# Row scores of a graph-attention layer: from transposes on TensorE to block turns on VectorE and a spread through memory, with new orders of the steps

## The chip, the core and the metric

The kernel runs on one core of a Trainium2 chip. The metric is the device time of one execution in microseconds, the median of five runs. Matrix products run on TensorE (PE; its weight loads are PEld), elementwise work on VectorE (DVE), ScalarE (ACT) and GpSimd (POOL); SyncE (SP) issues nearly all DMAs, in the order of its program. Every engine works through its own instructions in order and waits where an operand or a buffer isn't ready.

## What is computed

The input is x, 128 graphs of 128 nodes with 512 features, and a weighted adjacency adj per graph. Two layers follow each other, each with a residual. Cut to what matters:

```
h = relu(layernorm(x))                                # layer 0: attention over the graph
q, k, v = h Wq^T + bq, h Wk^T + bk, h Wv^T + bv       # 8 heads of 64
attn = softmax(q k^T / 8 * (adj + adj))               # per head, over keys
x = x + (attn v) Wo^T + bo
h = relu(layernorm(x))                                # layer 1: graph attention
Wh = h W
e = leaky_relu(Wh a[:512] + (Wh a[512:])^T, 0.2)      # a row score plus a column score
att = softmax(where(adj > 0.5, e, -9e15), axis=1)     # over the first index
x = x + elu(att Wh)
```

All is float32.

## The kernel before

Graphs go through in 64 pairs. For layer 0 two pairs make a group of four graphs; the projections q, k and v of a group are done with seven products instead of eight (a 2x2 block scheme: sums of token blocks and of weight blocks, `PRODUCTS`), called v0 to v6, q0 to q6, k0 to k6 and spread as "units" U1 to U11 over the two pairs before. A unit is four 128x128 by 256 matmuls (L249). Their results are moved out of PSUM by F (ACT, copy or bias) and A (DVE, add). Then, for each graph of a pair (suffix a and b): sc, the scores (L311); at, the weighting with adj (L318); mx, ex, rc, nm, the softmax; fl, bl, pl, which turn the shares in 32x32 blocks on DVE (L346), write them to memory and fetch them back in turned places (SP, L350 and L356); pc, the context (L375). o0 to o6 are the seven products of the output projection (L290), od their adds to x (L389).

Layer 1 of a pair: st (statistics, L159), pw (EPS and the power -0.5 on POOL, L163 and L164), nm and h2 (normalised h, L405), then four dot products per pair (L412): d00 and d10 give the row score of each node of the two graphs, d01 and d11 the column score, each against a vector of 512 (`us_sb`, `ut_sb`) that is W times one half of a, worked out once. The mask step needs, on every partition, the row scores of all 128 nodes along the free dimension. So pb (L421) turns the score column, broadcast to 128 columns, against the identity on TensorE, one transpose per graph, and wm (L427) reads pb in PSUM beside adjT. pr (leaky), m1, e1, sw finish the softmax; g0, g1 gather (L453), w0 to w6 are the products with W (L290), zc and wd collect them; ez, fa, fb (L476, L479, L482) make the elu and the residual over both graphs of the pair at once, so (L485) stores 512 KB.

Once, at the start: five weights of 1 MB each are loaded by one DMA each (Lv, Lq, Lk, Lo, Lw, L622), their block sums are made on DVE (W..0 to W..3, L134 to L140); bo and the two halves of a are loaded as rows broadcast to all partitions (Lc, Lu0, Lu1). ccp (L494) multiplies Wo with bv, broadcast to 128 columns, ccd adds bo: a constant row c that sh adds to x (L225). The first four pairs get their h by normalising rows (hn) and turning them on TensorE (tp, L188; ev, ACT). The biases bq, bk, bv come as columns on ACT's DMA queue.

No planner runs at build time. The order in which all engines' instructions are issued is written out in three lists: HEAD (first pairs, every step with its pair), ORDER (one period of the pairs 3 to 59; "pb:2" is the step pb of the pair two before the current one) and TAIL (last pairs, counted from the end). Each engine gets its instructions in the order of these lists, and SP its DMAs: a DMA that waits holds back all that stand behind it.

Of the kernel before, what the change touches and what calls it, by code (L numbers as in the profile page):

```python
# [13 lines left out]
P = 128  # L14
# [5 lines left out]
Q = 32  # L20
# [4 lines left out]
def kernel(  # L25
# [86 lines left out]
    bv_sb = column(bv, "bv")  # L112

# [3 lines left out]
    c_sb, us_sb, ut_sb = (const.tile([P, E], F32, name=name) for name in ("c", "u_src", "u_dst"))  # L117

    def load_row(dst, src, offset=0):
        nc.sync.dma_start(dst, bass.AP(tensor=src.tensor, offset=src.offset + offset, ap=[[0, P], [1, E]]))  # L120
# [32 lines left out]
    def row_stats(src, name):  # L153

        mv = small.tile([P, 2, 2], F32, name=name)

        def stats(i):
            st = small.tile([P, nc.vector.BN_STATS_DIM], F32, name="st")
            nc.vector.bn_stats(st, src[:, i, :])  # L159
            nc.vector.bn_aggr(mv[:, i, :], st)  # L160

        def power():
            nc.gpsimd.tensor_scalar_add(mv[:, :, 1], mv[:, :, 1], EPS)  # L163
            nc.gpsimd.tensor_tensor(mv[:, :, 1], mv[:, :, 1], mhalf.to_broadcast([P, 2]), OP.pow)  # L164

        return mv, stats, power
# [4 lines left out]
    def stats0(p, i):  # L171
        if p not in st0:
            st0[p] = row_stats(xs[p] if p < 3 else x0s[p], "mv0")
        st0[p][1](i)
# [185 lines left out]

    cxT = const.tile([P, 7, 2, S], F32, name="cxT")
# [34 lines left out]
    def centre1(p):  # L396
        mv = l1s[p][0]
        nmr = small.tile([P, 2], F32, name="nmr")
        nc.vector.scalar_tensor_tensor(nmr, mv[:, :, 0], -1.0, mv[:, :, 1], op0=OP.mult, op1=OP.mult)
        l1s[p] = mv, nmr  # L400
        h1s[p] = work.tile([P, 2, E], F32, name="h2"), small.tile([P, 2, 2], F32, name="ws")
# [7 lines left out]
    def dot1(p, i, k):  # L409
# [3 lines left out]
            junk, h2[:, i, :], 1.0, (us_sb, ut_sb)[k], op0=OP.mult, op1=OP.mult, accum_out=ws[:, i, k : k + 1]  # L413
        )

    def scores1(p):
        ws = h1s[p][1]

        pb = ps1.tile([P, 2, S], F32, name="pb", tag="ps1")
        for i in range(2):  # L420
            nc.tensor.transpose(pb[:, i, :], ws[:, i, 0:1].to_broadcast([P, P]), ident)  # L421
        pbs[p] = pb

    def mask1(p):

        wts[p] = work.tile([P, 2, S], F32, name="w", bufs=2)
# [7 lines left out]
    def maxima1(p):  # L434
        l1s[p] = small.tile([P, 2], F32, name="nmx1"), small.tile([P, 2], F32, name="sums1")
# [7 lines left out]
    def normalise1(p):  # L443
        w, (_, sums) = wts[p], l1s.pop(p)
        rs = small.tile([P, 2], F32, name="rs1")
# [27 lines left out]
    def elu(p):  # L473

        ezs[p] = work.tile([P, 2, E], F32, name="ez")
        nc.scalar.activation(ezs[p], zs[p], AF.Exp)  # L476

    def finish_a(p):
        nc.vector.scalar_tensor_tensor(xs[p], zs[p], 0.0, xs[p], op0=OP.max, op1=OP.add)  # L479

    def finish_b(p):
        nc.vector.scalar_tensor_tensor(xs[p], ezs.pop(p), 1.0, xs[p], op0=OP.min, op1=OP.add)  # L482
# [4 lines left out]
    ucol = const.tile([P, 2, C], F32, name="ucol")  # L487


    def product_c():  # L490
        onces["c"] = pm = ps1.tile([P, 2, E // 2], F32, name="pm", tag="ps1")
        for f in range(2):
            for c in range(C):
                nc.tensor.matmul(  # L494
                    pm[:, f, :], bv_sb[:, c : c + 1].to_broadcast([P, P]), wo_sb[:, 2 * (c // 2) + f, c % 2, :],
# [3 lines left out]
    def sum_c():  # L499
        pm = onces["c"].rearrange("p f k -> p (f k)")  # L500
        nc.vector.scalar_tensor_tensor(c_sb, pm, -1.0, c_sb, op0=OP.add, op1=OP.add)


    def dots_u(i, half):
        junk = work.tile([P, E], F32, name="junk")
        for c in (2 * half, 2 * half + 1):
            nc.vector.scalar_tensor_tensor(
                junk.rearrange("p (f k) -> p f k", f=2), w1_sb[:, 2 * half : 2 * half + 2, c % 2, :], 1.0,
                (us_sb, ut_sb)[i].rearrange("p (f k) -> p f k", f=2), op0=OP.mult, op1=OP.mult,
                accum_out=ucol[:, i, c : c + 1],  # L510
            )

    def turn_u(i):
        onces["u", i] = pu = ps1.tile([P, C, P], F32, name="pu", tag="ps1")
        for c in range(C):
            nc.tensor.transpose(pu[:, c, :], ucol[:, i, c : c + 1].to_broadcast([P, P]), ident)

    def keep_u(i):
        pu = onces["u", i].rearrange("p c k -> p (c k)")
        nc.scalar.activation((us_sb, ut_sb)[i], pu, AF.Copy, scale=1.0 if i else 1.0 / MASK)  # L520
# [11 lines left out]
    def listed(text, mark):  # L532
# [3 lines left out]
        lx@0 Lq@0 t0@-5 lx@1 Lo@0 Lk@0 Wq0@0 t1@-5 pp@0 t1@-4 lx@2 Lc@0 t0@-4 hn0@0 pp@1 Lv@0 hn1@0 tp0@0 Lw@0 tp1@0  # L536
        Lu0@0 ev0@0 hn1@1 ev1@0 hn0@1 tp1@1 Wq1@0 U6@-2 Wq2@0 tp0@1 ccp@0 ev0@1 t0@-3 F6@-2 t1@-3 ev1@1 Wk0@0 pp@2 l0@-2
        Wk2@0 la@-1 lt@0 Wk1@0 U5@-1 Lu1@0 hs2@-3 Wv0@0 hn0@2 U8@-2 ccd@0 hs0@-3 sh@0 U3@-1 t1@-2 tp0@2 F3@-1 la@0 U1@-1
        t0@-2 hs1@-3 pp@3 hn1@2 U7@-1 hs3@-3 hn0@3 hn1@3 U10@-2 cu01@0 F7@-1 l0@-1 ev0@2 Ww0@0 tp1@2 Wo0@0 U9@-1 ev1@2
        A8@-2 F10@-2 cu11@0 U1@-2 F9@-1 A5@-1 sh@1 tp0@3 U2@-1 tp1@3 F2@-1 U10@-1 ev0@3 A2@-1 ev1@3 hs0@-1 U4@-1 F10@-1  # L540
        Wv1@0 Wq3@0 t0@-1 U3@1 F4@-1 Ww1@0 hs1@-1 sca@0 t1@-1 scb@0 ata0@0 l0@0 s0@-1 ata1@0 U6@-1 mxa@0 Ww3@0 exa0@0
        U2@-2 Wv2@0 exa2@0 exa3@0 U8@-1 F1@-2 rca1@0 Wo2@0 nma2@0 exa1@0 U1@0 A9@-1 Wk3@0 rca0@0 t0@0 nma1@0 U3@-2
        nma3@0 A2@-2 nma0@0 t1@0 U4@-2 F3@-2 fla@0 l0@1 s0@0 f0@0 atb0@0 bla@0 U5@-2 atb1@0 Wv3@0 mxb@0 U11@-1 F5@-2
        exb3@0 U7@-2 A11@-1 exb1@0 A5@-2 exb0@0 cu00@0 U6@0 f0@1 pla@0 hs2@-1 Wo1@0 U2@0 F6@0 rcb0@0 A6@-1 F7@-2 exb2@0
        U9@-2 F1@0 rcb1@0 nmb3@0 F3@1 U10@0 A9@-2 lT@1 nmb2@0 cu10@0 nmb1@0 lT@0 sup0@0 scb@1 sua0@0 nmb0@0 sca@1 F10@0
        flb@0 U7@1 ata0@1 blb@0 ata1@1 A2@0 U5@1 F7@1 mxa@1 U9@1 Wo3@0 exa0@1 hd0@0 plb@0 exa2@1 exa1@1 pca@0 hs3@-1
        t0@1 U3@0 pea@0 rca0@1 hd1@0 nma1@1 exa3@1 U1@1 F3@0 rca1@1 t1@1 nma0@1 nma2@1 l0@2 s0@1 U2@1 nma3@1 la@1 fla@1
        U5@0 F2@1 atb0@1 bla@1 F9@1 hd0@1 o0@0 atb1@1 o1@0 mxb@1 pcb@0 pla@1 U4@1 peb@0 exb3@1 cs0@0 od0@0 exb1@1 cs1@0
        U8@0 A2@1 exb2@1 A5@1 exb0@1 cs2@0 U6@2 F5@0 A8@0 t0@2 t1@2 U4@0 od1@0 rcb1@1 rcb0@1 Ww2@0 nmb2@1 U8@1 nmb0@1
        nmb3@1 nmb1@1 U6@1 F4@1 flb@1 F6@2 hd1@1 U10@1 blb@1 hs0@1 cs3@0 o2@0 F10@1 A6@1 pca@1 od2@0 hs1@1 plb@1 sca@2  # L550
        pea@1 o4@0 ata0@2 ata1@2 o3@0 f0@2 od4@0 l0@3 mxa@2 U7@0 lt@1 od4c@0 A9@1 sup1@0 o5@0 sua1@0 exa1@2 o0@1 od5@0
        exa2@2 o1@1 exa0@2 o6@0 od0@1 st0@0 pcb@1 od6@0 st1@0 peb@1 scb@2 exa3@2 od1@1 pw@0 U11@1 cs0@1 rca1@2 rca0@2
        hs2@1 nma0@2 cs1@1 nma1@2 A5@0 s0@2 o2@1 nma2@2 nm@0 nma3@2 U1@2 F7@0 fla@2 h20@0 U9@0 atb0@2 F1@2 bla@2 h21@0
        atb1@2 mxb@2 U3@2 lT@2 A9@0 exb3@2 d00@0 exb2@2 U10@2 d01@0 pla@2 F3@2 od2@1 exb0@2 cs2@1 U5@2 hs3@1 A11@1 la@2
        d11@0 U4@2 F5@2 hd0@2 exb1@2 rcb1@2 rcb0@2 d10@0 o4@1 nmb3@2 nmb1@2 U8@2 od4@1 nmb2@2 A5@2 nmb0@2 flb@2 o3@1
        pb@0 U2@2 cs3@1 blb@2 od4c@1 wm@0 pr@0 U7@2 m1@0 o6@1 F7@2 plb@2 e1@0 o5@1 sw@0 U9@2 od6@1 hd1@2 g0@0 od5@1
        st0@1 g1@0 ge0@0 st1@1 A2@2
    """
    ORDER = """
        U1:0 A9:1 F10:1 pw:2 so:4 hs2:1 A1:8 ge1:3 F8:-4 gs0:3 w0:3 nm:2 w1:3 zc0:3 sca:0 F11:1 h20:2 wd1:3 gs2:3 scb:0  # L560
        h21:2 A4:8 ata0:0 ata1:0 pca:1 lx:1 hs1:1 pcb:1 mxa:0 pea:1 F1:0 U11:1 gs1:3 lT:0 exa1:0 A6:1 d00:2 U2:0 exa3:0
        d10:2 exa0:0 A8:1 d01:2 exa2:0 U3:0 rca0:0 d11:2 peb:1 nma0:0 A11:1 w2:3 rca1:0 F2:0 cs0:1 cs1:1 nma1:0 w3:3
        zc2:3 pb:2 nma2:0 U4:0 wm:2 nma3:0 cs2:1 A2:0 pr:2 gs3:3 F3:0 o0:1 fla:0 o1:1 atb0:0 bla:0 w4:3 A7:-9 A3:-1 m1:2
        f0:0 atb1:0 lt:1 U5:0 zc4:3 mxb:0 la:0 e1:2 sh:1 o3:1 wd4c:3 pla:0 w5:3 od0:1 od1:1 U6:0 zc5:3 F5:0 A10:7 A5:0
        exb2:0 sw:2 exb3:0 w6:3 exb0:0 rcb1:0 o2:1 wd6:3 exb1:0 cs3:1 g0:2 od2:1 nmb2:0 hs3:1 rcb0:0 nmb3:0 o4:1 fa:3
        nmb1:0 U7:0 nmb0:0 t1:0 ge0:2 od4:1 od4c:1 g1:2 F7:0 flb:0 ez:3 o5:1 blb:0 F6:0 o6:1 od5:1 F4:0 st0:1 U9:0 t0:0
        F9:0 od6:1 s0:0 U8:0 hd0:0 plb:0 hd1:0 U10:0 hs0:0 fb:3 st1:1 l0:-1
    """
    TAIL = """
        so@-8 w0@-7 F10@-5 A9@-5 pw@-6 w1@-7 hs1@-5 sca@-4 zc0@-7 ge1@-7 scb@-4 ata0@-4 lx@-5 nm@-6 pca@-5 ata1@-4  # L570
        h21@-6 gs0@-7 mxa@-4 pcb@-5 pea@-5 U6@-4 peb@-5 A6@-5 exa1@-4 gs1@-7 gs2@-7 exa3@-4 cs0@-5 hs2@-5 o0@-5 h20@-6
        o1@-5 exa0@-4 d01@-6 U3@-3 exa2@-4 wd1@-7 cs2@-5 rca1@-4 d10@-6 nma3@-4 w2@-7 d00@-6 F6@-4 rca0@-4 U8@-4 sh@-5
# [194 lines left out]
```

## Time and profile before

| what | us |
| --- | --- |
| median of five runs | 2367.5 (2366.54 to 2368.3) |
| the profiled execution | 2367.5 |
| its span, first to last instruction | 2365.7 |
| TensorE busy | 2339.8 |
| VectorE busy | 2005.5 |
| ScalarE busy | 1436.8 |
| row-score transposes pb, 128 of them, busy | 24.5 |
| share of the chain that ended last, on TensorE | 97% |

The page names a group of instructions by its line in the kernel, its engine, what it writes and what it reads. The busy time of matmuls contains their drain, which overlaps the next matmul, so a matmul's "mean ns" is longer than the time that it takes in a stream. The chain that ended last is followed back from the last instruction to whatever released each step; its durations are the times between steps.

### The profile page before, as it was taken

To read this page: it belongs to the slowest core of one execution; us is meant where nothing else is said; L and a number is where in the kernel's file an instruction comes from. 1 tells how busy PE (TensorE), PEld (TensorE's weight loads), DVE (VectorE), ACT (ScalarE), POOL (GpSimd) and SP (SyncE) were. 2 spreads that over 40 slices of the span, in tenths; PEclk is the share of its full clock that TensorE was granted. 3 is DMA by queue.
4 is the path that set the end of the run, shared out by engine and by line. 5 is a ranking of instruction groups with operands and counts; after the bars stand their busy time and mean duration, and the time that the engine had idled before them with its cause. 6 is when DMAs were issued, how large, how long until landed. Compare 5 with 4: busy or idle time off the path is not lost.

```text
span 2365.7 us, 40912 instructions
## 1 busy us (share of the span) xinstructions
PE 2339.8 (99%) x14264; PEld 2060.3 (87%) x14264; DVE 2005.5 (85%) x4037; ACT 1436.8 (61%) x4811; POOL 221.3 (9%) x323
## 2 busy tenths in 40 slices
PE   7999999999999999999999999999999999999997
PEld 6888888888888888888888888888888888888886
DVE  7788888888888888888888888888888888888887
ACT  3656566665566665655665666556656566665674
POOL 1000110101101101011011010010110100101000
PEclk9999999999999999999999999999999999999999
DMA  5445445444544454455454554544554545544432
GB/s 178 122 114 126 134 123 138 133 125 133 134 126 134 134 133 122 130 133 135 125 134 133 135 128 123 140 128 125 134 141 127 131 120 140 132 128 119 123 113 86
DMA packets 255277, 306.11 MB, mean 129 GB/s; under 512 B 21856, under 2 KB 181600, under 8 KB 254432
## 3 DMA queue, kind: packets, MB, share of 16 engines
q1 hardware_dynamic: 251568, 303.37, 46.7%
q8 instruction: 113, 1.85, 0.3%
q14 instruction: 92, 0.75, 0.1%
q0 software_dynamic: 1920, 0.13, 0.1%
q10 hardware_dynamic: 1584, 0.01, 0.0%
HBM read 202.64 MB, written 100.79 MB: 128 GB/s over the span
## 4 chain that ended last, share of the span: by engine, by line
PE 97%; DVE 2%; DMA 1%; issue 0%; ACT 0%; POOL 0%; SPq 0%; DVEq 0%; ACTq 0%; POOLq 0%
PE acc_a L249 28%; PE row_a L290 23%; PE acc_c L249 14%; PE row_c L290 9%; PE acc_b L249 7%; PE sc L311 5%; PE pc L375 5%; PE pg L453 5%; PE pb L421 1%; DMA wq<-in_wqT 0%; DVE junk L412 0%; PE pt L188 0%; DVE st L159 0%; DMA x<-in_x 0%; DVE x L482 0%
## 5 line engine op out<-in xcount | busy, mean ns | idle before, releaser
L330 ACT ACTIVATE at<-at,nmx 128x128 f32<-128x128 f32 x1024 | 396.3, 391 | 12.1 <-DVE nmx L325 9.6
L467 ACT COPY z<-row_a 128x256 f32<-128x256 f32 x256 | 94.7, 370 | 431.7 <-PE row_a L290 308.0
L339 ACT ACTIVATE at<-at,rs 128x128 f32<-128x128 f32 x1024 | 323.5, 393 | 4.0 <-DVE rs L334 3.9
L290 PE MATMUL row_a<-w,gT 128*128 128x256 f32 x1280 | 319.5, 380 | 1.7 <-ACT z L467 1.4
L290 PE MATMUL row_a<-wo,cxT 128*128 128x256 f32 x1280 | 318.8, 380 | 0.3 <-DVE cxT L147 0.3
L290 PEld LDWEIGHTS row_a<-w,gT 128*128 128x128 f32 x1280 | 242.2, 190 | 37.0 <-ACT z L467 2.6
L290 PEld LDWEIGHTS row_a<-wo,cxT 128*128 128x128 f32 x1280 | 234.0, 190 | 27.9 <-DVE cxT L147 0.5
L163 POOL TENSOR_SCALAR mv<-mv 128x2 f32<-128x2 f32 x128 | 30.5, 239 | 2090.6 <-DVE mv L160 2056.2
L266 ACT ACTIVATE kT<-acc_a,bk 128x256 f32<-128x256 f32 x256 | 107.0, 470 | 164.7 <-PE acc_a L249 163.3
L266 ACT ACTIVATE qT<-acc_a,bq 128x256 f32<-128x256 f32 x256 | 106.2, 469 | 164.2 <-PE acc_a L249 164.2
L330 ACT ACTIVATION_READ_ACCUMULATOR at<-at,nmx 128x1 f32 x1024 | 194.4, 190 | 0.0
L159 DVE BATCH_NORM_STATS2 st<-x 128x6 f32<-128x512 f32 x256 | 174.5, 682 | 8.3 <-DMA x<-in_x 6.1
L389 DVE TENSOR_TENSOR x<-row_a,x 128x256 f32<-128x256 f32 x320 | 133.1, 416 | 47.8 <-PE row_a L290 39.3
L318 DVE SCALAR_TENSOR_TENSOR at<-sc,adj 128x512 f32<-128x512 f32 x256 | 169.7, 684 | 4.6 <-PE sc L311 2.0
L346 DVE STREAM_TRANSPOSE tr<-at 128x1024 f32<-128x1024 f32 x128 | 158.2, 1236 | 9.4 <-ACT at L339 8.4
L325 DVE TENSOR_REDUCE nmx<-at 128x8 f32<-128x1024 f32 x128 | 155.8, 1217 | 3.2
L164 POOL TENSOR_TENSOR mv<-mv,mhalf 128x2 f32<-128x2 f32 x128 | 144.2, 1126 | 10.6
L453 PEld LDWEIGHTS pg<-w,h 128*128 128x128 f32 x1024 | 133.5, 192 | 7.0 <-issue 0.7
L311 PEld LDWEIGHTS sc<-kT,qT 64*128 64x128 f32 x2048 | 119.7, 188 | 21.2 <-issue 20.2
L453 PE MATMUL pg<-w,h 128*128 128x128 f32 x1024 | 134.3, 275 | 0.1
L290 PE MATMUL row_c<-w,gT 128*128 128x256 f32 x512 | 131.6, 380 | 1.0 <-DVE z L471 1.0
L311 PE MATMUL sc<-kT,qT 64*128 64x128 f32 x2048 | 132.5, 279 | 0.0
(126 smaller groups left out, 4893.5 us busy)
## 6 DMA issues: line engine op xcount, KB each, us to landing
blocks<-tr SPq DMA_DIRECT2D x128, 512.0 KB, 2.9
aT<-blocks SPq DMA_DIRECT2D x512, 128.0 KB, 3.1
x<-in_x SPq DMA_DIRECT2D x123, 512.0 KB, 3.9
out<-x SPq DMA_DIRECT2D x64, 512.0 KB, 5.6
hA<-in_xT SPq DMA_DIRECT2D x120, 256.0 KB, 4.1
mr<-rows SPq DMA_DIRECT2D x60, 256.0 KB, 4.6
adj<-in_adj SPq DMA_DIRECT2D x64, 128.0 KB, 4.9
adjT<-in_adjT SPq DMA_DIRECT2D x64, 128.0 KB, 4.9
```

What stands on the lines that cost most here:

```text
L159: nc.vector.bn_stats(st, src[:, i, :])
L164: nc.gpsimd.tensor_tensor(mv[:, :, 1], mv[:, :, 1], mhalf.to_broadcast([P, 2]), OP.pow)
L249: nc.tensor.matmul(acc[:, m, :], lhsT, rhs, start=fresh and m == 0 and c == 0, stop=c == 1, skip_group_check=True)
L266: nc.scalar.activation(dst(t, f)[:, m, :], a[:, m, :], AF.Identity, bias=bias[:, j : j + 1])
L290: nc.tensor.matmul(acc, left[:, la, c, :], w[:, wb, c, :], start=n in (0, 3) and c == 0, stop=c == 1, skip_group_check=True)
L311: nc.tensor.matmul(sc[s][:, j, :], qT[r, j, cols], kT[r, j, cols], start=True, stop=True)
L318: nc.vector.scalar_tensor_tensor(ats[b][0][:, k * C : (k + 1) * C, :], scs[b][k], QSCALE, adjs[p][:, i : i + 1, :].to_broadcast([P, C, S]) ...
L325: nc.vector.tensor_reduce(nmx, at, AX.X, OP.max, negate=True)
L330: nc.scalar.activation(at[:, j, :], at[:, j, :], AF.Exp, bias=nmx[:, j : j + 1], accum_out=sums[:, j : j + 1])
L339: nc.scalar.activation(at[:, j, :], at[:, j, :], AF.Copy, scale=rs[:, j : j + 1])
L346: nc.vector.transpose(trs[b], at.rearrange("p h (j k) -> p j h k", k=Q))
L453: nc.tensor.matmul(pg[:, c, :], h1s[p][0][:, i, c * P : (c + 1) * P], wts[p][:, i, :], start=True, stop=True)
```

## The change

The row scores of all pairs but the last two are no longer turned on TensorE. d00 and d10 write their sums into column 0 and column 32 of a zeroed tile of 128x64, `src_sb`. px turns that tile in 32x32 blocks on VectorE into the first 64 columns of the pair's w tile; partitions 0, 32, 64 and 96 then hold the scores in runs of 32. pd writes these runs to memory (SP, 1 KB), pv reads the 1 KB back on every partition (SP, 128 KB) into the w tile, and wm reads it there. For the last two pairs pb stays.

Each weight is loaded in two DMAs of 512 KB (blocks 0 and 2, blocks 1 and 3). The two halves of a come with one DMA; bo comes as a fourth column on ACT's queue; c is made as a column (matmuls with one moving column each) and turned into a row by four transposes (ccs, cch). For the first four pairs EPS is added on VectorE. Before the first step 24 transposes of the identity run on TensorE. The last pair's ez, fa, fb and so are cut in quarters (qe, qa, qb; three stores). Some small tiles have fewer buffers. HEAD, ORDER and TAIL are new throughout.

```diff
+    bo_sb = column(bo, "bo")
...
+    def load_weight(w, src, k):
+
+        nc.sync.dma_start(w[:, 0:4].rearrange("p (j k) c f -> p j k c f", k=2)[:, :, k], src.rearrange("p (j k) c f -> p j k c f", k=2)[:, :, k])
...
+            if soon:
+                nc.vector.tensor_scalar_add(mv[:, i, 1:2], mv[:, i, 1:2], EPS)
...
+    src_sb = const.tile([P, 2, Q], F32, name="src1")
+    nc.gpsimd.memset(src_sb, 0.0)
...
-            junk, h2[:, i, :], 1.0, (us_sb, ut_sb)[k], op0=OP.mult, op1=OP.mult, accum_out=ws[:, i, k : k + 1]
+            junk, h2[:, i, :], 1.0, u_sb[:, k, :], op0=OP.mult, op1=OP.mult, accum_out=ws[:, i, 1:2] if k else src_sb[:, i, 0:1]
...
-            nc.tensor.transpose(pb[:, i, :], ws[:, i, 0:1].to_broadcast([P, P]), ident)
+            nc.tensor.transpose(pb[:, i, :], src_sb[:, i, 0:1].to_broadcast([P, P]), ident)
...
+    def turn_scores1(p):
+
+        wts[p] = work.tile([P, 2, S], F32, name="w", bufs=2)
+        nc.vector.transpose(wts[p][:, 0, 0 : 2 * Q], src_sb.rearrange("p b q -> p (b q)"))
+
+    def send_scores1(p):
+        pbs[p] = dram.tile([2, P], F32, name="row1")
+        rows = wts[p][0:P:Q, 0, 0 : 2 * Q].rearrange("j (b q) -> j b q", q=Q)
+        nc.sync.dma_start(pbs[p].rearrange("b (j q) -> j b q", q=Q), rows)
+
+    def spread_scores1(p):
+        r = pbs[p]
+        pbs[p] = wts[p]
+        nc.sync.dma_start(wts[p].rearrange("p b s -> p (b s)"), r.rearrange("b p -> (b p)").partition_broadcast(P))
...
-                    pm[:, f, :], bv_sb[:, c : c + 1].to_broadcast([P, P]), wo_sb[:, 2 * (c // 2) + f, c % 2, :],
+                    pm[:, j : j + 1], wo_sb[:, 2 * (c // 2) + j // 2, c % 2, ms], bv_sb[:, c : c + 1],
...
+    def warm_up():
+
+        pu = ps1.tile([P, P], F32, name="warm", tag="ps1")
+        for _ in range(24):
+            nc.tensor.transpose(pu, ident, ident)
...
     HEAD = """
-        lx@0 Lq@0 t0@-5 lx@1 Lo@0 Lk@0 Wq0@0 t1@-5 pp@0 t1@-4 lx@2 Lc@0 t0@-4 hn0@0 pp@1 Lv@0 hn1@0 tp0@0 Lw@0 tp1@0
-        Lu0@0 ev0@0 hn1@1 ev1@0 hn0@1 tp1@1 Wq1@0 U6@-2 Wq2@0 tp0@1 ccp@0 ev0@1 t0@-3 F6@-2 t1@-3 ev1@1 Wk0@0 pp@2 l0@-2
-        Wk2@0 la@-1 lt@0 Wk1@0 U5@-1 Lu1@0 hs2@-3 Wv0@0 hn0@2 U8@-2 ccd@0 hs0@-3 sh@0 U3@-1 t1@-2 tp0@2 F3@-1 la@0 U1@-1
+        lx@0 lx@1 Lq1@0 Lq0@0 lx@2 Lk0@0 Lk1@0 Lv0@0 t1@-5 Lo0@0 t0@-5 pp@0 hn0@0 hn1@0 tp0@0 t0@-4 tp1@0 ev0@0 ev1@0
+        t1@-4 U6@-2 Wq0@0 pp@1 Wq1@0 t1@-3 U8@-2 hn0@1 l0@-2 Wq2@0 Lv1@0 hn1@1 tp0@1 Lo1@0 U3@-1 Lw1@0 t0@-3 ev0@1 Lu@0
+        Wq3@0 pp@2 tp1@1 hn1@2 U5@-1 ev1@1 hn0@2 F6@-2 Wk0@0 hs0@-3 F3@-1 U1@-2 Wk1@0 hs1@-3 hs2@-3 U10@-2 tp0@2 F10@-2
+        U7@-1 t1@-2 t0@-2 U2@-1 Wv0@0 F7@-1 pp@3 Wk3@0 F1@-2 A8@-2 ev0@2 U9@-1 hn0@3 Wv1@0 hn1@3 hs3@-3 tp0@3 l0@-1
...
     ORDER = """
-        U1:0 A9:1 F10:1 pw:2 so:4 hs2:1 A1:8 ge1:3 F8:-4 gs0:3 w0:3 nm:2 w1:3 zc0:3 sca:0 F11:1 h20:2 wd1:3 gs2:3 scb:0
-        h21:2 A4:8 ata0:0 ata1:0 pca:1 lx:1 hs1:1 pcb:1 mxa:0 pea:1 F1:0 U11:1 gs1:3 lT:0 exa1:0 A6:1 d00:2 U2:0 exa3:0
-        d10:2 exa0:0 A8:1 d01:2 exa2:0 U3:0 rca0:0 d11:2 peb:1 nma0:0 A11:1 w2:3 rca1:0 F2:0 cs0:1 cs1:1 nma1:0 w3:3
-        zc2:3 pb:2 nma2:0 U4:0 wm:2 nma3:0 cs2:1 A2:0 pr:2 gs3:3 F3:0 o0:1 fla:0 o1:1 atb0:0 bla:0 w4:3 A7:-9 A3:-1 m1:2
-        f0:0 atb1:0 lt:1 U5:0 zc4:3 mxb:0 la:0 e1:2 sh:1 o3:1 wd4c:3 pla:0 w5:3 od0:1 od1:1 U6:0 zc5:3 F5:0 A10:7 A5:0
-        exb2:0 sw:2 exb3:0 w6:3 exb0:0 rcb1:0 o2:1 wd6:3 exb1:0 cs3:1 g0:2 od2:1 nmb2:0 hs3:1 rcb0:0 nmb3:0 o4:1 fa:3
-        nmb1:0 U7:0 nmb0:0 t1:0 ge0:2 od4:1 od4c:1 g1:2 F7:0 flb:0 ez:3 o5:1 blb:0 F6:0 o6:1 od5:1 F4:0 st0:1 U9:0 t0:0
-        F9:0 od6:1 s0:0 U8:0 hd0:0 plb:0 hd1:0 U10:0 hs0:0 fb:3 st1:1 l0:-1
+        U1:0 fa:4 ge0:3 pw:2 hs1:1 fb:4 g1:3 nm:2 lT:0 so:4 sca:0 h20:2 scb:0 h21:2 ata0:0 ge1:3 ata1:0 pca:1 mxa:0
+        pcb:1 pea:1 d00:2 F1:0 U11:1 exa1:0 A6:1 A8:1 U2:0 exa0:0 d10:2 exa3:0 t0:0 px:2 exa2:0 gs0:3 rca0:0 w0:3 pd:2
+        A11:1 A10:8 A1:8 nma1:0 rca1:0 w1:3 gs1:3 t1:0 nma2:0 gs2:3 o0:1 s0:0 zc0:3 nma0:0 lx:1 wd1:3 U3:0 nma3:0 hs3:1
+        d01:2 fla:0 o1:1 F3:0 peb:1 w2:3 atb0:0 bla:0 atb1:0 w3:3 zc2:3 mxb:0 F2:0 la:-1 w4:3 pv:2 gs3:3 lt:2 U5:0 zc4:3
+        cs0:1 cs2:1 cs1:1 F5:0 sh:1 pla:0 exb3:0 U4:0 exb2:0 exb0:0 rcb1:0 od0:1 l0:-1 U7:0 od1:1 exb1:0 f0:-1 wd4c:3
+        F8:-8 A5:0 nmb3:0 A2:0 F4:0 U8:0 nmb2:0 A3:3 rcb0:0 d11:2 F11:-4 nmb0:0 cs3:1 nmb1:0 A7:-9 o2:1 w5:3 od2:1 wm:2
+        U6:0 A4:-4 flb:0 zc5:3 pr:2 m1:2 blb:0 hd0:0 e1:2 w6:3 F6:0 o4:1 F7:0 o3:1 od4:1 wd6:3 U9:0 od4c:1 sw:2 F9:0
+        plb:0 hd1:0 ez:3 o5:1 hs2:0 hs0:0 o6:1 od5:1 U10:0 A9:0 st0:1 od6:1 g0:2 st1:1 F10:0
...
     TAIL = """
...
-        ge1@-1 ez@-2 gs2@-1 w1@-1 gs0@-1 gs1@-1 w3@-1 zc0@-1 wd1@-1 fb@-2 w2@-1 gs3@-1 zc2@-1 so@-2 w4@-1 zc4@-1 w5@-1
-        wd4c@-1 w6@-1 zc5@-1 wd6@-1 fa@-1 ez@-1 fb@-1 so@-1
+        wd6@-2 ge0@-1 fa@-2 w0@-1 ge1@-1 ez@-2 gs2@-1 w1@-1 gs0@-1 gs1@-1 w3@-1 zc0@-1 wd1@-1 gs3@-1 w2@-1 fb@-2 zc2@-1
+        qa00@-1 qe00@-1 so@-2 w4@-1 qb00@-1 so@-3 zc4@-1 w5@-1 wd4c@-1 qa11@-1 qe11@-1 w6@-1 qb11@-1 zc5@-1 qe01@-1
+        qs1@-1 qa01@-1 wd6@-1 qb01@-1 qe10@-1 qa10@-1 qs0@-1 qb10@-1 qs2@-1
...
+        if p < N - 2:
+            table.pop("pb")
+            table |= {
+                "px": lambda: turn_scores1(p), "pd": lambda: send_scores1(p), "pv": lambda: spread_scores1(p),
+            }
+        if p == N - 1:
+            for step in ("ez", "fa", "fb", "so"):
+                table.pop(step)
...
+        warm_up()
         for step, p in HEAD:
```

## The prediction

> **What bounds the kernel now.** I read the page first: engines, slices and the chain that ended last.
>
> ```profile
> span 2365.7 us, 40912 instructions
> PE 2339.8 (99%) x14264; PEld 2060.3 (87%) x14264; DVE 2005.5 (85%) x4037; ACT 1436.8 (61%) x4811; POOL 221.3 (9%) x323
> PE   7999999999999999999999999999999999999997
> PE 97%; DVE 2%; DMA 1%; issue 0%; ACT 0%; POOL 0%; SPq 0%; DVEq 0%; ACTq 0%; POOLq 0%
> ```
>
> TensorE is busy for all but 25.9 us, and 97% of the chain is TensorE running one matmul after the other. Only the first and the last of the forty slices have a gap. Since a busy PE need not be a PE that has work, I asked for the busy time by stage (window, length, PE, PEld, DVE, ACT, POOL, granted clock, DMA share, GB/s).
>
> ```profile
> 0.00:12.50 12.50, 0.00 (x0) 0.00 (x0) 4.43 (x11) 1.28 (x1) 2.04 (x10) 1.00 0.81 280
> 12.50:110.00 97.50, 97.50 (x548) 84.74 (x548) 74.46 (x137) 48.90 (x162) 9.23 (x15) 1.00 0.46 144
> 110.00:1000.00 890.00, 889.80 (x5441) 785.65 (x5440) 760.21 (x1534) 546.72 (x1843) 85.41 (x122) 1.00 0.47 129
> 1000.00:2000.00 1000.00, 1000.00 (x6137) 883.26 (x6136) 858.72 (x1723) 613.77 (x2061) 98.74 (x140) 1.00 0.49 131
> 2340.00:2366.00 26.00, 15.50 (x71) 11.02 (x69) 15.43 (x32) 9.94 (x21) 0.82 (x1) 0.92 0.16 61
> ```
>
> From 12.5 to 2250 us TensorE has no gaps. In that stretch only work taken from TensorE itself shortens the kernel. A second test: in the chain a unit of a projection takes 1.73 us and half a unit 0.86; per pair there are 10.5 units (18.13), seven o and seven w products (6.05 each), sc 1.99, pc 1.90, pg 1.78, pb 0.22 and 0.19 of a slower first unit after pc: 36.31 us. The scores of every second pair begin 72.61 us apart (249.50, 322.11), so 36.31 a pair. Nothing is left over.
>
> The row-score transposes, from the groups by form and from the chain of the end (start, duration, what):
>
> ```profile
> L421 PE MATMUL pb<-ident,ws 128*128 128x128 f32 x128 | 24.5, 273 | 1.2 <-DVE junk L412 1.2
> L427 DVE SCALAR_TENSOR_TENSOR w<-adjT,pb 128x256 f32<-128x256 f32 x64 | 26.9, 420 | 87.3 <-PE pb L421 87.3
> 2230.10 0.22 PE pb L421 x2
> ```
>
> The 273 ns is the length of one matmul with its drain; in the stream two of them take 0.22 us. The 87.3 us that VectorE waits for pb cost nothing in themselves, because VectorE does not set the end.
>
> The start, from the timeline, and the last pieces of the chain:
>
> ```profile
> 12.50 2.82 PE L188 MATMUL pt<-ident,hn 128*128 128x128 f32 x12 [12.50 <-DVE hn L181]
> 15.16 2.73 PE L249 MATMUL acc_a<-hA,wq 128*128 128x256 f32 x8
> 8.84 0.69 DVE L134 TENSOR_TENSOR wq<-wq 128x512 f32<-128x512 f32 x1 [3.92 <-DMA wq<-in_wqT]
> 2358.89 1.23 DVE x L479
> 2360.22 1.23 DVE x L482
> ```
>
> At the start VectorE sits 3.92 us behind a weight sum that waits for the 1 MB load of wq, while x of pair 0 has been there since 4.0 us. At the end two full-width VectorE operations and a 512 KB store follow the last matmul.
>
> **What the Trainium skill says.** "TensorE: Matmul & The Clock Gate", Part 1 (the HAM clock gate): the array starts at half rate and comes to full rate after some 3.4 us of activity. The trace agrees: the first 12 transposes take 0.235 us each where later ones take 0.11 (four in 0.44), and the first unit takes 2.56 where later ones take 1.73. "VectorE: DVE Perf Modes", The three transpose paths: VectorE turns 32x32 blocks only, into SBUF. So the turned scores lie in four partitions and must still be spread. "DMA: Bandwidth & Descriptors", Anatomy of one DMA: a fit for GpSimd's queue puts some 2 us of each DMA down as fixed, mostly waiting for the write receipt; the trace has 2.9 us to landing even for the 512 KB store of blocks. Same page, Two DMAs through the same engine are not ordered: the spread must wait for the store's completion on the issuing queue. No DMA of the kernel before is that small on SP.
>
> **The change, part by part** (minus is gain).
>
> 1. **pb leaves TensorE for 62 of 64 pairs.** 62 x 0.22 = **-13.6 us**, all in a stretch where PE is full. Bounds -12.4 to -15 (0.20 to 0.24 by rounding and by the switch to the next matmul).
>
> 2. **What replaces it.** VectorE: one 128x64 transpose per pair. The 128x1024 one takes 1236 ns, so between 0.08 and 0.25 us (small VectorE operations take 0.15); I take 0.15, and against it VectorE loses the 1.4 us a pair that it waited for pb. At 86% busy (859 of 1000 us) it has some 5 us a pair over. SP: two more DMA issues per pair at about 0.43 us. In the new order pd is followed by w1, o0, U3, o1, w2, w3, w4 on PE before pv: 0.86 x 6 + 1.73 = 6.9 us, against a landing of 2 to 6 us (blocks 2.9; the tiny GpSimd store rows 6.4). Behind pd and pv on SP stand lx, bla, la and then lt, pla; pla is needed only by the next period's pca, over 15 us later. From pv to the mask wm PE does U5, U4, U7, U8, o2, w5: 8.6 us, against 4.6 us for mr, the nearest broadcast, twice as large. From wm to g0 there are another 10 us of PE for 3.4 us of mask chain. So **0**; if the cover is gone, wm blocks VectorE in order (rival A). The new order's PE sequence has the same products with the same switches (sc, sc, pc, pc, then a unit); I put its own effect at 0, from -1 to +4 us over all pairs.
>
> 3. **The start.** Loss before: 12.50 idle, 2.82 - 1.31 = 1.51 in the slow transposes, 2.56 - 1.73 = 0.83 in the slow first unit: 14.8 us. After: x of pair 0 is in at about 4.5 (the first half at 4.0); statistics 2 x (0.69 + 0.18 + 0.15 for the added EPS) to 6.6; POOL's power 0.71 to 7.3; hn0, hn1 0.54 each; turns and ev1 (0.60) to 9.5. The first unit needs blocks 0 and 2 of wq, the fourth half-megabyte in the queue: 2.1 MB, and by the windows of one us the DMAs had moved 2.0 MB by 9.0. So the unit starts at about 9.8, with 0.87 us of turns done: loss 8.9, gain 5.9. The 24 warm-up transposes (at most 24 x 0.235 = 5.6 us, from about 1.5) end before hn0. I give 1.0 back for what comes late then: SP waited at the start for bq, bk and bv (1.2, 3.2, 4.7 us), there is now a fourth such column, and wv is needed at about 17 us instead of 34. **-4.9**, from -1.5 to -7.
>
> 4. **The constant c.** product_c took 3.46 us as 16 wide matmuls. Now 32 with one column: not below pc's 0.064 us each (64-column weights), hardly above pg's 0.11 (128-column weights), at the worst the 0.19 of an exposed weight load: 2.0, 3.5, 6.1. I take 3.5, plus 0.44 for turning the column: **+0.4**, from -1.0 to +3.
>
> 5. **The end.** After the last add (0.43): before, 1.23 + 1.23 and gaps to 2361.45; now qb01, qa10, qb10 at 0.42 each with the exponential beside the first: about 1.3 us, so -1.2. The last store is 128 KB instead of 512 KB, whose data ran from about 2362 to 2364: -1.1. **-2.3**, from -1 to -4. Other PE gaps of the end (0.9, 1.9 and 2.8 us in the last three windows) can move either way by 2: 0.
>
> Sum: -13.6 + 0 - 4.9 + 0.4 - 2.3 = **-20.4**. The profiled execution took 2367.5 us, 1.8 around its span of 2365.7; it is also the median of the five, so 2367.5 - 20.4 = **2347**.
>
> **Rivals.**
> A, slower: the spread comes late. SP issues in order; pv waits for pd to land, with a store of 512 KB between them, and wm stands in VectorE's order. If store and spread together take over the 15.5 us from pd to wm plus about 2 that VectorE can make up, PE starves in every pair. From 0.33 us a pair (20.4 / 62) the kernel is no longer faster; with 0.6 it is 2347 + 37 = **2384**. Against: both landings by the nearest rows sum to 7.5 to 11 us, and DMA is half idle (0.47 to 0.49).
> B: small stalls. The old list left no gap; a new one with 0.1 us a pair (+6) and 3 us more at the start gives **2356**.
> C: TensorE's freed time is not gained, since VectorE (85%) becomes the bound of some stretch, so that the removal does nothing: only start and end are left, -6.8, **2361**. Against: VectorE's 31 us of 36 a pair.
>
> **How the numbers follow.** Main case 0.72, B 0.14, C 0.07, A 0.07. Main case's ends: 2340 (-15, -7, -1, -4 together) to 2353. The range 2340 to 2357 takes in B; C, A and the outer ends of the main case, some 0.2, are left out. About 0.2% (4.7 us) is what a measurement tells from no change. Faster: main, B and nearly half of C, 0.89; same 0.04; slower 0.07.
>
> **What would show it.** PE without gaps in the middle, with a period of 36.1 instead of 36.3 a pair: part 1. pb twice two, a new transpose of about 0.15 us, wm without idle for the spread: part 2. The first unit of q near 9.8 us at full rate: part 3. The pm group at about 0.11 spacing: part 4. Last matmul to span's end 5 us instead of 7.4: part 5. Idle of VectorE at wm put down to the DMA, with gaps in PE, would make the prediction wrong.

## The result, and the profile after

The changed kernel takes 2363.6 us (median of 27 runs, 2359.6 to 2366.4) against 2367.8 before (47 runs): a ratio of 0.9981, 95% interval 0.9976 to 0.9986. It is faster by 0.19%, 4.2 us where 20.4 were forecast, and lies outside the range of 2340 to 2357. The profiled execution took 2364.1 us with a span of 2362.3. From its page:

```profile
span 2362.3 us, 41114 instructions
PE 2337.3 (99%) x14184; PEld 2066.3 (87%) x14184; DVE 2001.0 (85%) x4113; ACT 1457.2 (62%) x4815; POOL 257.0 (11%) x320
PE   9999999999999999999999999999999999999998
PE 89%; DVE 4%; POOL 3%; ACT 3%; issue 1%; DMA 0%; POOLq 0%; ACTq 0%; SPq 0%; DVEq 0%
```

TensorE's share of the time is 99% as before, and it did lose work: 14264 instructions became 14184 although some were added. But its share of the chain fell from 97% to 89%, and VectorE, POOL and ScalarE, which had 2% of it together, have 10%. So something now waits in turn for all three. The stages tell where (window, length, then PE and the rest as before):

```profile
0.00:12.50 12.50, 7.47 (x35) 6.65 (x36) 6.12 (x17) 2.48 (x3) 2.60 (x10) 0.83 0.86 256
12.50:110.00 97.50, 97.50 (x540) 85.35 (x539) 73.15 (x138) 46.74 (x162) 12.20 (x14) 0.95 0.43 143
110.00:1000.00 890.00, 885.35 (x5402) 784.84 (x5401) 758.29 (x1561) 555.84 (x1840) 99.46 (x122) 1.00 0.45 133
1000.00:2000.00 1000.00, 994.49 (x6082) 882.11 (x6081) 853.79 (x1748) 623.00 (x2060) 114.84 (x137) 1.00 0.45 133
```

Between 110 and 2000 us TensorE had 0.2 us without work before; now it has 4.65 + 5.51 = 10.2. The clock column shows a second thing: 0.95 in the window from 12.5 to 110, where it was 1.00. (The column doesn't show every slow stretch: in the kernel before it read 1.00 from 12 to 18 us too, where the first transposes took 0.235 us each instead of 0.11 and the first unit 2.56 us instead of 1.73.)

The waits name the gap. These are the lines of the waits of all engines, with who waited, for whom, the total, the count and the longest:

```profile
PE pc L388 <- ACT gT L487: 10.9, 28, 0.4
ACT h L418 <- DVE nmr L412: 148.7, 60, 3.1
POOL mv L172 <- DVE mv L166: 2010.5, 123, 34.3
```

One wait on TensorE, 28 times 0.39 us, in every second pair: pc, the first context product, waits for ScalarE's copy of gathered rows, a step of another pair. ScalarE in turn waits for nmr, 60 times. This is one such place in the timeline (start, length, engine, line and operation, and in brackets the idle time before it):

```profile
863.22 0.69 DVE L165 BATCH_NORM_STATS2 st<-x 128x6 f32<-128x512 f32 x1
...
864.04 1.19 DVE L511 SCALAR_TENSOR_TENSOR x<-z,x 128x1024 f32<-128x1024 f32 x1
864.30 1.02 POOL L172 TENSOR_SCALAR mv<-mv 128x2 f32<-128x2 f32 x1 [22.98 <-DVE mv L166]
...
865.34 1.22 DVE L515 SCALAR_TENSOR_TENSOR x<-ez,x 128x1024 f32<-128x1024 f32 x1
865.40 1.75 POOL L173 TENSOR_TENSOR mv<-mv,mhalf 128x2 f32<-128x2 f32 x1
...
866.04 1.05 PE L481 MATMUL pg<-w,h 128*128 128x128 f32 x8
...
867.03 2.06 PE L320 MATMUL sc<-kT,qT 64*128 64x128 f32 x32
867.18 0.16 DVE L412 SCALAR_TENSOR_TENSOR nmr<-mv 128x2 f32<-128x2 f32 x1 [0.62 <-POOL mv L173]
867.44 1.52 ACT L418 ACTIVATE h<-x,nmr,mv 128x512 f32<-128x512 f32 x2 [2.33 <-DVE nmr L412]
...
868.86 0.56 ACT L487 COPY gT<-pg 128x512 f32<-128x512 f32 x1
869.48 1.73 PEld L388 LDWEIGHTS pc<-aT,v 128*64 128x64 f32 x32 [0.59 <-ACT gT L487]
869.48 1.97 PE L388 MATMUL pc<-aT,v 128*64 128x128 f32 x32 [0.40 <-ACT gT L487]
```

The gather g1 ends at about 867.0; its copy ge1 has nothing to wait for from then on. Yet it starts at 868.86, since h20 and h21 stand before it on ScalarE, and these wait for the statistics, for two POOL steps and for nmr. pc uses nothing that ge1 makes. But both use a bank of PSUM, TensorE's result memory, and the banks that the built program gives to its tiles show that in every second pair the first pc gets the bank that pg of g1 held. Which tile gets which bank is settled when the program is built, from the order of the lists. (In the middle of the kernel before, pc always followed a sc in its bank.) So pc starts 2.45 us after sc instead of 1.99. The period of two pairs is 72.67 us (sc at 1230.34 and 1303.01); it was 72.61 (249.50 and 322.11). Before, in the chain, then after, in the timeline:

```profile
249.50 1.99 PE sc L311 x32
322.11 1.99 PE sc L311 x32
324.10 1.90 PE pc L375 x32
1230.34 2.06 PE L320 MATMUL sc<-kT,qT 64*128 64x128 f32 x32
1303.01 2.06 PE L320 MATMUL sc<-kT,qT 64*128 64x128 f32 x32
```

The 0.44 us that two pb took have gone into a wait of 0.47.

What replaces pb holds TensorE up nowhere. From the groups by form:

```profile
L439 DVE STREAM_TRANSPOSE w<-src 128x64 f32<-128x64 f32 x62 | 13.3, 215 | 0.1
L455 DVE SCALAR_TENSOR_TENSOR w<-adjT,w 128x256 f32<-128x256 f32 x62 | 25.7, 415 | 0.0
```

And from the DMA issues (count, size, median us to landing):

```profile
w<-row SPq DMA_DIRECT2D x62, 128.0 KB, 3.5
```

The turn takes 215 ns (150 were taken, at most 250), the spread lands in 3.5 us, and the mask doesn't wait for it at all.

**The theories.** Theory bank: the wait for ge1, brought in by the new lists (ge1 behind h20 and h21 on ScalarE, and another order of the PSUM banks), has eaten the gain of pb. Its rival, theory loop: VectorE, POOL and ScalarE hold the period of two pairs at 72.6 us, whatever TensorE does; that both periods are so nearly equal speaks for it. For the start and the constant c a third question is the clock.

### The profile page after: what moved, and what is told of

Same layout as the page of the kernel before. It is cut to its first block, busy times and chain, and to the rows that moved or that the text cites. A ratio compares the mean times of both kernels' runs of the same rounds, so it can differ in the third digit from the quotient of the medians.

```text
span 2362.3 us, 41114 instructions
## 1 busy us (share of the span) xinstructions
PE 2337.3 (99%) x14184; PEld 2066.3 (87%) x14184; DVE 2001.0 (85%) x4113; ACT 1457.2 (62%) x4815; POOL 257.0 (11%) x320
## 4 chain that ended last, share of the span: by engine, by line
PE 89%; DVE 4%; POOL 3%; ACT 3%; issue 1%; DMA 0%; POOLq 0%; ACTq 0%; SPq 0%; DVEq 0%
PE acc_a L258 26%; PE row_a L299 23%; PE acc_c L258 12%; PE row_c L299 8%; PE acc_b L258 7%; PE pc L388 5%; PE sc L320 3%; PE pg L481 3%; POOL mv L173 2%; ACT h L418 2%; DVE st L165 2%; POOL mv L172 1%; DVE x L402 1%; DVE v L279 1%; ACT gT L487 1%
## 5 line engine op out<-in xcount | busy, mean ns | idle before, releaser
L299 PE MATMUL row_a<-wo,cxT 128*128 128x256 f32 x1280 | 328.4, 380 | 0.3 <-DVE cxT L153 0.3
L172 POOL TENSOR_SCALAR mv<-mv 128x2 f32<-128x2 f32 x124 | 79.2, 639 | 2032.7 <-DVE mv L166 2010.5
L299 PEld LDWEIGHTS row_a<-wo,cxT 128*128 128x128 f32 x1280 | 242.6, 190 | 34.3 <-DVE cxT L153 0.6
L418 ACT ACTIVATE h<-x,nmr,mv 128x512 f32<-128x512 f32 x128 | 97.5, 808 | 151.0 <-DVE nmr L412 148.7
L425 DVE SCALAR_TENSOR_TENSOR junk<-h,u 128x512 f32<-128x512 f32 x256 | 173.1, 676 | 0.6
L388 PE MATMUL pc<-aT,v 128*64 128x128 f32 x2048 | 127.5, 277 | 11.0 <-ACT gT L487 10.9
L173 POOL TENSOR_TENSOR mv<-mv,mhalf 128x2 f32<-128x2 f32 x128 | 131.0, 1024 | 30.9 <-DVE mv L168 20.6
```

The source lines that it names most:

```text
L299: nc.tensor.matmul(acc, left[:, la, c, :], w[:, wb, c, :], start=n in (0, 3) and c == 0, stop=c == 1, skip_group_check=True)
L388: nc.tensor.matmul(pc[s * D : (s + 1) * D, j, :], vs[b // G][:, b % G, head * D : (head + 1) * D], aT[:, :, s * C + j, :], start=True, sto ...
L425: nc.vector.scalar_tensor_tensor(junk, h2[:, i, :], 1.0, u_sb[:, k, :], op0=OP.mult, op1=OP.mult, accum_out=ws[:, i, 1:2] if k else src_sb ...
```

## The experiments

All were timed against the kernel before on the same chip.

**ge1 moved ahead of h20.**

```diff
-U1:0 fa:4 ge0:3 pw:2 hs1:1 fb:4 g1:3 nm:2 lT:0 so:4 sca:0 h20:2 scb:0 h21:2 ata0:0 ge1:3 ata1:0 ...
+U1:0 fa:4 ge0:3 pw:2 hs1:1 fb:4 g1:3 nm:2 ge1:3 lT:0 so:4 sca:0 h20:2 scb:0 h21:2 ata0:0 ata1:0 ...
```

> The changed kernel with one step moved in ORDER: ge1 (ScalarE's copy of the second gather out of PSUM) stands before h20 and h21 instead of behind them. Theory bank: in every second pair pc of the next pair takes the PSUM bank that the second gather g1 held, ge1 frees it, and ge1 stands on ScalarE behind h20 and h21, which wait for statistics, POOL and nmr; pc starts 0.47 us late, which eats the 0.44 us that two pairs save by the two pb. Then the wait of pc for gT (10.9 us in 28 times) goes, two pairs take 72.17 us instead of 72.66, and the median falls by 28 x 0.49 = 13.7 to about 2350. Theory loop (VectorE, POOL and ScalarE hold the period of two pairs at 72.6, whatever TensorE does): the wait turns up at another place, the median stays above 2361.

Measured: 2351.2 us, ratio 0.9927 (0.9915 to 0.9940). The timeline of the same place:

```profile
857.94 1.05 PE L481 MATMUL pg<-w,h 128*128 128x128 f32 x8
...
858.92 2.06 PE L320 MATMUL sc<-kT,qT 64*128 64x128 f32 x32
859.03 0.59 ACT L487 COPY gT<-pg 128x512 f32<-128x512 f32 x1 [2.03 <-PE pg L481]
...
859.51 1.52 ACT L418 ACTIVATE h<-x,nmr,mv 128x512 f32<-128x512 f32 x2
...
860.91 1.97 PE L388 MATMUL pc<-aT,v 128*64 128x128 f32 x32
```

The copy starts when the gather ends, pc follows sc after 1.99 us, two pairs take 72.21 us (sc at 1219.99 and 1292.20), and TensorE is busy for all of 110 to 2000 us. One step moved on one engine is worth 12.4 us. The wait turned up nowhere else: theory loop falls. The move also changed the banks: in the built program of this run the first pc gets the bank of g1 in every pair, and still it never waits. So the shared bank costs nothing by itself; what costs is that the copy which frees it comes late.

**pb put back, with ge1 early.**

```diff
-        if p < N - 2:
+        if p < N - 2 and not 6 <= p <= 52:
             table.pop("pb")
...
-... w4:3 pv:2 gs3:3 ...
+... w4:3 pb:2 pv:2 gs3:3 ...
```

> As ge1_first, and the transposes pb on TensorE are put back for the pairs 6 to 52 (47 of them), in the middle of the period, without px, pd and pv. Measures what pb costs where TensorE has no gap. Theory bank: 47 x 0.22 = 10.3 us more than ge1_first, about 2360. Theory loop: the same as ge1_first within 2 us, since TensorE isn't what sets the period.

Measured: 2361.5 us, 10.2 more than without pb, 0.218 us for each of 47 pairs. That agrees with the price of 0.22.

**pb put back in the changed kernel as it is.** The same edit without the move of ge1.

> The changed kernel in its own order (ge1 behind h20 and h21), with pb put back on TensorE for the pairs 6 to 52, without their px, pd and pv. Theory bank: pb lies outside the stretch from o6 to pc in which the copy ge1 is late, so the wait stays and pb comes on top: 2363.6 + 47 x 0.22 = 2373.9, that is slower than the kernel before. Theory loop: the period of two pairs is held at 72.6 by another engine and TensorE has room: 2364.

Measured: 2374.8 us, ratio 1.0024 (1.0014 to 1.0035), and the wait is there as before:

```profile
PE pc L388 <- ACT gT L487: 11.4, 29, 0.4
```

This is the clearest run of the study: with pb still in it the new order is slower than the kernel before by 6.3 us. TensorE's time counts in full, and so does the wait on top of it.

**The old order without pb.**

```diff
-        pb = ps1.tile([P, 2, S], F32, name="pb", tag="ps1")
-        for i in range(2):
-            nc.tensor.transpose(pb[:, i, :], ws[:, i, 0:1].to_broadcast([P, P]), ident)
-        pbs[p] = pb
+        pbs[p] = c_sb[:, 0 : 2 * S].rearrange("p (b s) -> p b s", b=2)
```

> The kernel before in its own order, with pb left out for all pairs: the mask reads the constant row c in the place of the turned row scores, so the row scores are left out of the result. Shows whether the old order gains what pb takes. Theory bank: in the old order ge1 stands before h20 on ScalarE, so nothing takes the place of pb: 64 x 0.22 = 14 us less than before, 2353.8. Rival: VectorE or another engine takes it back: 2362 or more.

This kernel leaves the row scores out of its result. Measured: 2354.1 us, 13.6 less than before (64 pairs, 0.213 each). In the old order nothing takes the place of pb, although one PSUM tile per pair is gone there too; in the built program pc still follows sc in its bank, and in the trace pc waits for no copy.

**Why h20 is late: fa and fb behind nm.** In the place above, POOL's EPS step took 1.02 us and its power 1.75; in most places of the kernel before the same two take 0.22 and 0.73. fa and fb run on VectorE at that moment.

```diff
-U1:0 fa:4 ge0:3 pw:2 hs1:1 fb:4 g1:3 nm:2 lT:0 so:4 ...
+U1:0 ge0:3 pw:2 hs1:1 g1:3 nm:2 fa:4 fb:4 lT:0 so:4 ...
```

> The changed kernel with ge1 left behind h20 and h21; instead fa and fb of the pair before (two VectorE operations of 1.2 us with two SBUF inputs) stand behind nm in ORDER, so that they don't run beside POOL's two steps and nmr doesn't stand behind them. Theory: POOL's EPS step takes about 0.22 us instead of 1.02 and its power 0.72 instead of 1.0 to 1.75, h20 starts 2 us earlier, ge1 with it, and pc waits no more: about 2350. If what matters is only that ge1 stands behind h20, whatever the chain before h20 takes, pc still waits: 2362.

Measured: 2359.8 us, ratio 0.9965 (0.9952 to 0.9979). Half a miss. The timeline, and the line of the waits:

```profile
1225.59 0.22 POOL L172 TENSOR_SCALAR mv<-mv 128x2 f32<-128x2 f32 x1 [22.78 <-DVE mv L166]
...
1225.89 0.72 POOL L173 TENSOR_TENSOR mv<-mv,mhalf 128x2 f32<-128x2 f32 x1
1226.64 0.16 DVE L412 SCALAR_TENSOR_TENSOR nmr<-mv 128x2 f32<-128x2 f32 x1 [1.23 <-POOL mv L173]
...
1227.34 1.05 PE L481 MATMUL pg<-w,h 128*128 128x128 f32 x8
...
1228.43 1.52 ACT L418 ACTIVATE h<-x,nmr,mv 128x512 f32<-128x512 f32 x2 [2.04 <-PE pg L481]
...
1229.86 0.56 ACT L487 COPY gT<-pg 128x512 f32<-128x512 f32 x1
1230.47 1.73 PEld L388 LDWEIGHTS pc<-aT,v 128*64 128x64 f32 x32 [0.28 <-ACT gT L487]
PEld pc L388 <- ACT gT L487: 16.3, 57, 0.3
```

POOL is fast, and nmr is ready at 1226.8. But now h20 waits for pg: h2 has one buffer, which the gather g1 of the pair before still reads. So behind h20 the copy can't start earlier than 1.5 us after the gather's end, and sc covers only 2.0 of the 2.1 us that h and copy take. pc waits 0.16 us in every pair instead of 0.47 in every second. (It is every pair because in the built program of this run, too, the first pc gets the bank of g1 in each of them.) The lateness had two sources, the chain through POOL and the buffer of h2; the place of ge1 behind h20 lets both through to TensorE.

**The constant c with 128 moving columns.** In the changed kernel's profile the group of 32 one-column matmuls and what follows it look like this in the chain (start, duration, what):

```profile
33.34 4.57 PE pm L531 x32
37.91 3.62 PE acc_a L258 x8
41.53 2.17 PE acc_c L258 x8
```

The granted clock, by windows of 2 us (window, length, PE and the rest, clock third from the end):

```profile
34.00:36.00 2.00, 2.00 (x18) 2.00 (x18) 0.00 (x0) 0.72 (x2) 0.00 (x0) 0.87 0.00 0
36.00:38.00 2.00, 2.00 (x10) 2.00 (x11) 0.06 (x1) 0.00 (x0) 0.00 (x0) 0.50 0.00 0
38.00:40.00 2.00, 2.00 (x5) 1.59 (x6) 1.90 (x6) 0.00 (x0) 0.00 (x0) 0.50 0.00 0
40.00:42.00 2.00, 2.00 (x6) 1.60 (x5) 1.97 (x6) 0.00 (x0) 1.58 (x3) 0.50 0.45 128
```

PE counts as busy throughout, and the clock is halved. A unit of 1.73 us takes 3.62. The theory is that the single moving column of these matmuls brings the clock down; its rival is another cause, such as the idle time at the start.

```diff
...
-                    pm[:, j : j + 1], wo_sb[:, 2 * (c // 2) + j // 2, c % 2, ms], bv_sb[:, c : c + 1],
+                    pm[:, j, :], wo_sb[:, 2 * (c // 2) + j // 2, c % 2, ms], bv_sb[:, c : c + 1].to_broadcast([P, P]),
...
```

> The changed kernel, with the 32 one-column matmuls of product_c given 128 moving columns (bv broadcast) instead of one; the sum reads one column of them. Theory clock: [...]with 128 columns the group takes 3.5 us instead of 4.57 and the unit behind it 1.73 instead of 3.62 and the half one 1.73 instead of 2.17: -3.4 us where the clock fell, and the spread of the runs (2359.6 to 2366.4) shrinks: median about 2360.3. Rival: the clock falls for another reason (the idle stretch before the first turn): median 2362.5, only the group gets shorter.

Measured: 2361.2 us (2360.5 to 2362.9), 2.4 less than the changed kernel; the clock is 1.00 throughout from 30 to 110 us. The group and what follows it, in the timeline (with their drain):

```profile
33.66 3.74 PE L531 MATMUL pm<-bv,wo 128*128 128x128 f32 x32
37.24 1.89 PE L258 MATMUL acc_a<-wv,hA 128*128 128x256 f32 x8
38.96 1.89 PE L258 MATMUL acc_c<-wv,hS 128*128 128x256 f32 x8
```

In the chain the three take 3.57 + 1.73 + 1.73 instead of 4.57 + 3.62 + 2.17 us: 3.3 less, close to the 3.4 of the forecast. The profiled execution is nevertheless only 1.3 us shorter, for two other reasons: the group began 0.5 us later, and near the end, from 2340.9 to 2344.9 us, the clock was at 0.57 on average, which it was not in the changed kernel and which cost about 1.4 us. Nor does the narrow group bring the clock down every time: of the five profiles with it four show the fall, and in the fifth, that of ge1_first, it took 3.47 us at full clock. None of the six profiles with 128 columns shows it, although the slow stretch at the start is there in most of them; so the rival falls. Together with ge1:

> ge1 before h20 and the wide matmuls of product_c together. Theory: the two gains add, the clock never falls after 16 us, and the runs lie close together as the good ones of ge1_first do: 2347.8 plus or minus 0.7. If the clock still falls in some runs, median 2351 as in ge1_first.

Measured: 2348.9 us, the four runs within 0.8 us of each other where the changed kernel's 27 spread over 6.7. The gains add. The forecast was 1.1 us lower because it started from ge1_first's profiled execution, in which the clock was at half from about 10.8 to 14.2 us; in this one it was so from about 9.2 to 16.1.

**The warm-up.** Both on top of ge1_and_pm.

```diff
-        warm_up()
         for step, p in HEAD:
```

> As ge1_and_pm, without the 24 transposes at the start. In the profiles so far the clock was at half from about 9 to 15.5 us in spite of them. Theory: they gain at most the 0.8 us of the first turns: 0 to +1 us against ge1_and_pm. If they do what the prediction gave them: +2 us.

Measured: 2348.6 us: the 24 transposes gain nothing. With 48:

```diff
-        for _ in range(24):
+        for _ in range(48):
```

> As ge1_and_pm, with 48 transposes at the start instead of 24, so that TensorE is busy from 1.4 to about 8.5 us, until the first turns. Theory: the clock stays full, the first unit takes 1.73 us instead of 3.4 to 3.7 and what follows is no longer slow: -2 to -3 us, 2345. If the clock falls in the gap of 1.6 us before the first unit anyway: the same as ge1_and_pm.

Measured: 2346.6 us, ratio 0.9910 (0.9896 to 0.9923), the lowest of all. In the timeline the first unit takes 1.99 us with its drain (3.73 in the changed kernel; later units take 1.89):

```profile
1.44 8.25 PE L562 MATMUL warm<-ident 128*128 128x128 f32 x48 [1.44 <-POOL ident masks.py:199]
9.53 1.04 PE L197 MATMUL pt<-ident,hn 128*128 128x128 f32 x8
11.30 1.99 PE L258 MATMUL acc_a<-hA,wq 128*128 128x256 f32 x8 [0.74 <-ACT hA L200]
```

Two tries to go further failed. In the first (40 transposes, blocks 0 and 2 of wq first), TensorE stood still for 1.3 and 1.1 us before and after the first turns, and the clock was at 0.50 in the window from 12 to 14 us:

> As ge1_pm_warm48 with 40 transposes instead of 48, so that they end with the first turns, and blocks 0 and 2 of wq loaded before blocks 1 and 3, since the first unit needs the former. Theory: the first unit starts at about 10.5 us instead of 11.3 and the clock holds: 2345.8. If the clock falls in the gap before it: 2348.

Measured: 2347.4 us. In the second (44 transposes) the wq loads went ahead of x of pair 1:

> As ge1_pm_warm48 with 44 transposes, and the two loads of wq issued before x of pair 1 (blocks 0 and 2 first). In the profiles so far the wq loads were issued only when the bias bq had landed, at 4.3 us, and the last landed at about 11.2. Theory: they are issued by 3 us, land by about 9.5, the first unit waits for nothing but its own turns and starts at about 10.3 instead of 11.3 with the clock full: 2345.6. If x of pair 1 then comes late, or the clock falls in a gap: 2347 or more.

Measured: 2347.6 us. The first unit started at 10.43 us at full clock, as hoped, but x of pair 1 then landed at 10.1 us; TensorE waited 1.0 us for its turn and 0.5 for a block sum.

## Why the prediction was wrong

1. **pb leaves TensorE: right.** 0.22 us a pair was priced; 0.218 (47 pairs back) and 0.213 (64 pairs out) were measured. That TensorE's time sets the middle also held, as the run with pb in the new order shows.

2. **What replaces it: right for px, pd and pv, wrong for the order.** The step that failed is the sentence "The new order's PE sequence has the same products with the same switches (sc, sc, pc, pc, then a unit); I put its own effect at 0, from -1 to +4 us over all pairs." I compared TensorE's sequence with itself and did not follow what releases its PSUM banks. The lists stood in the text: ge1 ahead of h20 before, behind it after. With the wait the order's own effect was +12.4 us (changed kernel against ge1_first). The range given, -1 to +4, did not hold it. None of the rivals had this mechanism. Rival A put the wait on the spread, for which nothing waits; B had stalls of the right kind, but 0.1 us a pair where 0.22 was measured, and named no cause; C, that another engine holds the period, came nearest with its 2361, but by luck: putting pb back refutes it.

3. **The start: half.** Forecast -4.9. The first unit started at 11.43 us instead of 9.8 and was slower than before (3.73 us against 2.56): 11.43 - 0.87 + (3.73 - 1.73) = 12.6 us lost against 14.8, so -2.3. Two terms were too small: x of pair 0 was complete at 5.15 us, not 4.5, and the eight turns took 1.98 us instead of 0.87, since the clock had fallen. A third was hidden behind them: the wq loads were issued only at 4.3, when the bias bq had landed. Here they came before the unit was ready; in ge1_first the last one landed at 11.25 and was what the unit waited for. The 24 transposes did not keep the clock. The Trainium skill, "TensorE: Matmul & The Clock Gate", Part 1, says that idle time brings half rate back after a window of some 3.4 us. The trace agrees that it comes back, but not with the window: the idle stretches here (2.9 us after the transposes, 0.7 before the unit) are each shorter, and the clock was at half from about 8.2 us, 2.3 us after the last transpose.

4. **The constant c: the work right, the consequence missed.** At full clock the 32 matmuls take 3.47 us, against 3.5 estimated. That the clock would be halved for what follows was not considered: 4.57 + 0.44 + (3.62 - 1.73) + (2.17 - 1.73) = 7.3 us against 3.46 before, +3.9 in the profiled execution instead of +0.4, beyond the upper bound of 3.

5. **The end: right.** The last matmul group ends at 2357.26, 5.0 us before the span's end, where it was 7.4: -2.3. The other gaps of TensorE after 2300 us shrank from 5.6 to 3.9, which I had put at 0.

The sum by the traces: two pairs +0.05 instead of -0.44, 28 times, +1.4; the six other pairs -1.3; start -2.3; c +3.9; end -2.3; other gaps -1.7: -2.3, against 3.4 that the span fell; 1.1 us are not traced. With the wait and the narrow matmuls mended, the kernel takes 2348.9 us, 1.9 above the forecast of 2347, and with the wait alone mended 2351.2, inside the range: had the order been neutral, as the sum assumed, the range would have held. That it comes so near to 2347 is in part luck, since the start gave 2.6 us less than forecast and the gaps at the end 1.7 more.

## What to carry to other kernels

When work is taken off a full engine, follow also what that engine's buffers wait for: for each PSUM tile, the last reader of its bank, and what stands before that reader on its own engine. A step that only frees a buffer belongs ahead of steps that wait for a long chain, even if nobody seems to want its result yet. And a gain that vanishes almost to the hundredth is no proof of a bound elsewhere: put the work back, and see whether it costs.

## What the runs showed of the hardware

- Matmuls with one moving column keep TensorE busy in the profile (2.00 of 2.00 us), and yet the granted clock fell to 0.50 within their stretch and stayed there from about 35.5 to 42.3 us. It fell so in four of five profiles; with 128 moving columns in none of six. Why is open.
- POOL's 128x2 step took 1.02 us instead of 0.22 and the power up to 1.75 instead of 0.73 while VectorE ran operations on two full-width SBUF tiles; with these moved away it was 0.22 and 0.72 again in the place shown.
- 24 warm-up transposes followed by 2 to 3 us without work gained nothing (2348.9 us with them, 2348.6 without); 48 that ran until the first work gained 2.4 us. With 40, and gaps of 1.3 and 1.1 us behind them, the clock was halved again.
- The clock column read 1.00 at the start of the kernel before and of ge1_pm_no_warm, where the first unit took 2.56 and 3.75 us instead of 1.73. Half rate at the very start shows in the durations, not in this column.
